# A depthwise 7x7 convolution on TensorE: sixteen small tiles reading the input in place

## The chip, the cores and the metric

The kernel runs on one core of a Trainium2 chip. The metric is the device time of one execution in microseconds (us). A run's engines are TensorE (PE, with its weight loads shown as PEld), VectorE (DVE), ScalarE (ACT), GpSimd (POOL) and SyncE (SP, which only issues transfers here). All data are float32.

## What is computed

The input is 32 images of 96 channels of 56 x 56. Two layers follow each other: a ConvNeXt block (depthwise 7x7 convolution, layer norm over the channels, an MLP of 96 to 384 to 96 with an exact GELU, a residual), and a second layer (depthwise 5x5 convolution, SiLU, a selective scan over the 3136 tokens of an image).

```python
def block(x, conv_w, conv_b, ln_g, ln_b, w1, b1, w2, b2, layer_scale):
    h = depthwise_conv7(x, conv_w) + conv_b              # padding 3
    h = transpose(h, (0, 2, 3, 1))
    h = (h - mean(h)) * rsqrt(var(h) + 1e-5) * ln_g + ln_b   # over the 96 channels
    h = gelu(h @ w1 + b1) @ w2 + b2
    return transpose(h, (0, 3, 1, 2)) * layer_scale + x
def scan_layer(x, ...):
    x = silu(depthwise_conv5(x) + conv_b)                # padding 2
    ...                                                  # projections, softplus, two cumulative sums
```

## The kernel before

Four stages run one after the other, each with its own pools in SBUF and PSUM: first convolution, MLP, second convolution, scan. They hand tensors over in DRAM: `conv1_d` (the convolved channels), `rstd_d` (the norm's reciprocal deviation for each token), `block_d` (the block's output, laid out for the second convolution), `conv2_d`, `du_d`.

**First convolution (L141 to L363).** The images are taken as two halves j of 16 images; a row of an input tile is one image row, with 16 x 56 = 896 values of 16 images behind each other. One job is one channel (the last 16 channels are done half by half): 112 jobs. `load_x` (L156) brings 56 rows of each half. The convolution in the vertical direction is a product with a banded matrix of taps (56 input rows to 56 output rows). Two columns are done together: the even and odd columns of the input stand in `xq` above each other on partitions 0 to 55 and 64 to 119, so that 120 rows are contracted and 112 outputs (two columns x 56 rows) come out. To fill `xq`, every half of a channel is copied out of the loaded tile with a step of two: one copy on POOL or DVE (L328) and one on ACT (L329). Then four horizontal offsets t are accumulated for each half (L334), 8 matmuls of 120 x 112 x 448 a channel. The weights are slices of a tile `wt`, read from the padded table `taps1_d` with two loads a job (`taps_of`, L306), with a step of four elements between columns.

ACT evicts the result with its bias (L343) into `ht`, POOL issues two stores into `conv1_d` (L347), and for the norm DVE subtracts the first channel (L356), adds to a sum (L357), ACT squares (L358), and DVE adds to the sum of squares (L359). `finish_norm(j)` (L126) makes the reciprocal deviation of one half and stores it. The small weights of the later stages are prepared beside the jobs (`beside`, L302); some of them hold a PSUM bank for a few jobs.

**MLP (L369 to L485).** The tokens of 4 image rows of one half and 32 channels make a tile of 128 partitions (`hts`); there are 28 groups n of 4 rows and two parts s (even or odd columns) in each. `hidden` (L413) runs four row tiles of TensorE, 32 x 128 each, `result` (L436) four column tiles, 128 x 32 each. `result` adds bias and residual with two DVE operations of 224 (L451), each picking every fourth column of the input tile `x` and every second value of PSUM, into `ot`, whose last part decides when POOL issues four stores into `block_d` (L463). `normalise` (L410) multiplies a group by `rstd`. In the program's order, the first group's loads come after all first-convolution jobs; a scheduler moves unpinned instructions ahead where buffers and queues allow, while those in `pin(...)` keep the order in which they are written.

**Second convolution and scan (L492 to L868).** The second convolution runs four column tiles of TensorE with a contiguous moving operand, and DVE puts its columns back in order. The scan is DVE's: two scans and one multiply for each of 192 units. Neither stage is touched.

Of the kernel before, what the change touches and what calls it, by code (L numbers as in the profile page):

```python
# [16 lines left out]
ROWS = B2 * H  # L17
# [6 lines left out]
WP = 128  # L24
W2 = W // 2
MP = 64
P1 = (K1 + 1) // 2
# [3 lines left out]
RW = 32  # L31
QP = QW + 1
# [6 lines left out]
EPS = 1e-9  # L39
APART = 16  # L40
# [7 lines left out]
def convnext_then_scan_kernel(  # L48
# [30 lines left out]
    conv1_d = dram.tile([C, ROWS, COLS], F32, name="conv1_d")  # L79
# [3 lines left out]
    rstd_d = dram.tile([ROWS, COLS], F32, name="rstd_d")  # L83
    taps1_d = dram.tile([C, 3 * WP * P1], F32, name="taps1_d")
# [22 lines left out]
    KR = MP + H  # L107
    PQ = HALF

# [8 lines left out]

    front = ctx.enter_context(ExitStack())
    stats = front.enter_context(tc.tile_pool(name="stats", bufs=1))  # L120
    first = stats.tile([ROWS, B2, HALF], F32, name="first")
    acc1 = stats.tile([ROWS, B2, HALF], F32, name="acc1")
    acc2 = stats.tile([ROWS, B2, HALF], F32, name="acc2")
    sq = stats.tile([ROWS, B2, HALF], F32, name="sq")

    def finish_norm(j):  # L126

        a1, a2 = acc1[:, j], acc2[:, j]
        nc.vector.tensor_mul(sq[:, j], a1, a1)
        nc.vector.scalar_tensor_tensor(  # L130
            a2, in0=sq[:, j], scalar=-1.0 / C, in1=a2, op0=ALU.mult, op1=ALU.add
        )
        nc.vector.tensor_scalar(a2, a2, 1.0 / C, 0.0, ALU.mult, ALU.max)
        nc.scalar.activation(a2, a2, AF.Sqrt, bias=eps_t[:ROWS], scale=1.0)
        nc.vector.reciprocal(a1, a2)
        for s in range(2):
            nc.gpsimd.dma_start(
                rstd_d[j * H : (j + 1) * H, s * PQ : (s + 1) * PQ], a1[s * H : (s + 1) * H]
            )

    with tc.tile_pool(name="c1", bufs=3) as pool, tc.tile_pool(  # L141
        name="c1k", bufs=1
    ) as keep, tc.tile_pool(name="prep", bufs=1) as prep, tc.tile_pool(
        name="c1_ps", bufs=4, space=PSUM
    ) as psum:
        wts = [keep.tile([128, 2, H * P1], F32, name=f"wt1_{i}") for i in range(5)]
        xqs = [keep.tile([128, B2, BI, W2 + 3], F32, name=f"xq_{i}") for i in range(3)]
        jobs = [(c, (0, B2)) for c in range(C - APART)]
        jobs += [(c, (j, j + 1)) for j in range(B2) for c in range(C - APART, C)]


        kt1 = prep.tile([C, K1, K1], F32, name="kt1")
        nc.sync.dma_start(kt1, c1w.rearrange("c (i j) -> c i j", j=K1))
        xts: dict = {}

        def load_x(n):  # L156
            c, js = jobs[n]
            xts[n] = pool.tile([128, COLS], F32, name=f"xt1_{n}", tag="xt")
            for j in range(*js):
                nc.sync.dma_start(xts[n][MP * j : MP * j + H], x[c, j * H : (j + 1) * H])  # L160
# [14 lines left out]
        c1b_t = across(c1b, ROWS, C, "c1b_t", const)  # L175
        pad = prep.tile([C, 3, WP, P1], F32, name="pad1")
        nc.vector.memset(pad, 0.0)
        at = H - 1 - K1 // 2
        for i in range(3):
            for t in range(P1):  # L180
                j = 2 * t + 1 - i
                if j in range(K1):
                    nc.vector.tensor_copy(pad[:, i, at : at + K1, t], kt1[:, :, j])
        nc.sync.dma_start(taps1_d, pad.rearrange("c d p t -> c (d p t)"))
        for t in wts + xqs + [acc1, acc2]:
            nc.vector.memset(t, 0.0)
# [119 lines left out]
        def taps_of(n):  # L306

            c, wt = jobs[n][0], wts[n % len(wts)]
            for s in range(2):
                taps = bass.AP(  # L310
                    taps1_d.tensor, taps1_d.offset + (c * 3 + 1 - s) * WP * P1,
                    [[P1, H], [WP * P1, 2], [1, H * P1]],
                )
                nc.sync.dma_start(wt[MP * s : MP * s + H], taps)

        for n in range(4):
            taps_of(n)
        for n, (c, js) in enumerate(jobs):
            if n + 4 < len(jobs):
                taps_of(n + 4)  # L320
            if n + 2 < len(jobs):
                load_x(n + 2)

            xq, xt = xqs[n % len(xqs)], xts.pop(n)
            for j in range(*js):
                xv = xt[MP * j : MP * j + H].rearrange("p (i r s) -> p s i r", i=BI, s=2)
                copy = nc.vector.tensor_copy if j else nc.gpsimd.tensor_copy
                copy(xq[:H, j, :, 2 : W2 + 2], xv[:, 1])  # L328
                nc.scalar.copy(xq[MP:KR, j, :, 1 : W2 + 1], xv[:, 0])  # L329
            wv = wts[n % len(wts)].rearrange("p o m -> p (o m)").rearrange("p (q t) -> p t q", t=P1)  # L330
            ps = bank(f"ps1_{n}")[:ROWS, :, :PQ]
            for t in range(P1):
                for j in range(*js):
                    nc.tensor.matmul(  # L334
                        ps[:, j].rearrange("p (i r) -> p i r", i=BI),
                        lhsT=wv[:KR, t],
                        rhs=xq[:KR, j, :, t : t + W2],
                        start=(t == 0),
                        stop=(t == P1 - 1),
                    )  # L340
            half = slice(*js)
            ht = pool.tile([ROWS, B2, HALF], F32, name=f"ht_{n}", tag="ht") if c else first
            nc.scalar.activation(  # L343
                ht[:, half], ps[:, half], AF.Identity, bias=c1b_t[:, c : c + 1], scale=1.0
            )
            for s in range(2):
                nc.gpsimd.dma_start(  # L347
                    conv1_d[c, js[0] * H : js[1] * H, s * PQ : (s + 1) * PQ].rearrange(
                        "(j m) q -> m j q", m=H
                    ),  # L350
                    ht[s * H : (s + 1) * H, half],
                )
            if c:

                dt = pool.tile([ROWS, B2, HALF], F32, name=f"dt_{n}", tag="dt")
                nc.vector.tensor_sub(dt[:, half], ht[:, half], first[:, half])  # L356
                nc.vector.tensor_add(acc1[:, half], acc1[:, half], dt[:, half])  # L357
                nc.scalar.activation(dt[:, half], dt[:, half], AF.Square)  # L358
                nc.vector.tensor_add(acc2[:, half], acc2[:, half], dt[:, half])  # L359
            if n >= 3 and beside:  # L360
                beside.pop(0)()
            if n == C + 1:
                finish_norm(0)  # L363
# [4 lines left out]

    with tc.tile_pool(name="mlp_ot", bufs=1) as pool_o, tc.tile_pool(  # L369
        name="mlp_g", bufs=14  # L370
    ) as pool_g, tc.tile_pool(name="mlp", bufs=2) as pool, tc.tile_pool(
        name="mlp_h", bufs=3, space=PSUM
    ) as ps_h, tc.tile_pool(name="mlp_o", bufs=2, space=PSUM) as ps_o:
        blocks = C // CB
        rts: dict = {}
        hts: dict = {}
        xts: dict = {}
        gts: dict = {}

        ots = [  # L380
# [532 lines left out]
```

## Time and profile before

| | us |
|---|---|
| median of three runs | 3596.53 (3595.88 to 3597.94) |
| the profiled execution | 3600.45 |
| its span, first to last instruction | 3598.7 |
| mean granted TensorE clock in it | 0.832 |

The profile shows this one execution: for each engine its busy time, groups of equal instructions with their mean duration, and for an engine's idle time the instruction that ended it. Matmuls overlap in TensorE, so the mean duration of one (541 ns) is longer than the distance between two. The transfers by queue:

```profile
q1 hardware_dynamic: 263168, 671.96, 57.9%
q0 software_dynamic: 29632, 80.27, 7.1%
q10 hardware_dynamic: 16904, 38.70, 2.8%
```

Columns: packets, MB, and the time of the packets as a share of 16 DMA engines over the span. q1 is what SP issues, q0 what POOL issues (`conv1_d`, `rstd_d`, `block_d`), q10 what ACT issues. The issues that the change touches, with the number of issues, the size of each, and for POOL's the time to landing:

```profile
block_d<-o POOLq DMA_DIRECT2D x336, 120.0 KB, 5.7
xt<-in_x_dram SPq DMA_DIRECT2D x192, 196.0 KB
x<-in_x_dram SPq DMA_DIRECT2D x336, 112.0 KB
h<-conv_d SPq DMA_DIRECT2D x84, 448.0 KB
```

### The profile page before, as it was taken

To read this page: it belongs to the slowest core of one execution; us is meant where nothing else is said; L and a number is where in the kernel's file an instruction comes from. 1 tells how busy PE (TensorE), PEld (TensorE's weight loads), DVE (VectorE), ACT (ScalarE), POOL (GpSimd) and SP (SyncE) were. 2 spreads that over 40 slices of the span, in tenths; PEclk is the share of its full clock that TensorE was granted. 3 is DMA by queue.
4 is the path that set the end of the run, shared out by engine and by line. 5 is a ranking of instruction groups with operands and counts; after the bars stand their busy time and mean duration, and the time that the engine had idled before them with its cause. 6 is when DMAs were issued, how large, how long until landed. Compare 5 with 4: busy or idle time off the path is not lost. (4 is left out here: it accounts for less than half of the span.)

```text
span 3598.7 us, 46673 instructions
## 1 busy us (share of the span) xinstructions
PE 3053.6 (85%) x17290; PEld 1288.2 (36%) x17290; DVE 2666.7 (74%) x1820; ACT 2352.2 (65%) x2168; POOL 1969.5 (55%) x1284
## 2 busy tenths in 40 slices
PE   8999998999999999899957777777777778777775
PEld 5777775333333333333312222222222222222221
DVE  6666666333333333699959999999999999999998
ACT  4555555333333333588868888888888887888884
POOL 2333343222222222000049899999999998999996
PEclk9999999999999999999966667667666666767666
DMA  6665555444444443699978787778877877877873
GB/s 185 194 179 168 173 168 170 154 158 158 158 157 156 160 157 93 201 283 286 287 222 299 271 266 255 283 253 270 282 256 259 290 255 253 283 255 267 281 259 122
DMA packets 309931, 793.92 MB, mean 221 GB/s; under 512 B 126840, under 2 KB 188304, under 8 KB 285160
## 3 DMA queue, kind: packets, MB, share of 16 engines
q1 hardware_dynamic: 263168, 671.96, 57.9%
q0 software_dynamic: 29632, 80.27, 7.1%
q10 hardware_dynamic: 16904, 38.70, 2.8%
q8 instruction: 137, 2.24, 0.3%
q14 instruction: 90, 0.74, 0.1%
HBM read 555.05 MB, written 235.74 MB: 220 GB/s over the span
## 5 line engine op out<-in xcount | busy, mean ns | idle before, releaser
L711 POOL TENSOR_TENSOR rep<-rep,bt 128x1568 f32<-128x1568 f32 x192 | 674.4, 3513 | 379.8 <-DMA rep<-du_d 379.8
L740 POOL TENSOR_TENSOR hs<-hs,ct 128x1568 f32<-128x1568 f32 x191 | 669.4, 3505 | 102.4 <-DVE hs L728 89.0
L721 DVE TENSOR_TENSOR_SCAN pv<-rep,pv 128x1568 f32<-128x1568 f32 x192 | 664.5, 3461 | 42.8 <-ACT rep L707 24.9
L431 ACT ACTIVATE g<-ph,b1p_t 128x896 f32<-128x896 f32 x336 | 320.0, 1004 | 512.4 <-PE ph L421 512.4
L451 DVE SCALAR_TENSOR_TENSOR o<-po,b2r_t,x 128x224 f32<-128x224 f32 x336 | 190.8, 609 | 567.9 <-PE po L440 567.9
L334 PE MATMUL ps<-xq,wt 120*112 120x448 f32 x1536 | 584.1, 541 | 20.9 <-DMA wt<-taps_d 17.5
L463 POOL DMA_DIRECT2D block_d<-o x336 | 183.1, 552 | 659.2 <-DVE o L451 627.9
L334 PEld LDWEIGHTS ps<-xq,wt 120*112 120x112 f32 x1536 | 429.8, 280 | 173.4 <-issue 22.2
L421 PE MATMUL ph<-h,w1r_t 32*128 32x448 f32 x4032 | 437.8, 558 | 23.7 <-DVE h L411 21.3
L639 PE MATMUL pz<-xs,wd_t 96*96 96x392 f32 x512 | 277.0, 706 | 172.6 <-ACT du L647 126.8
L440 PE MATMUL po<-g,w_t 128*32 128x448 f32 x4032 | 413.1, 543 | 0.0
L758 PE MATMUL py<-hs,sel_t 128*32 128x392 f32 x1536 | 327.5, 682 | 62.7 <-POOL hs L740 62.7
L686 PE MATMUL pk<-bn,pick_t 8*128 8x392 f32 x1024 | 288.5, 683 | 90.7 <-ACT y L767 78.5
L724 DVE SCALAR_TENSOR_TENSOR pv<-pv,rep 128x1568 f32<-128x1568 f32 x192 | 345.6, 1800 | 22.6 <-POOL rep L711 1.6
L533 PE MATMUL ps<-xq,wt 128*32 128x448 f32 x3072 | 309.3, 548 | 38.7 <-DMA xq<-block_d 32.8
L728 DVE TENSOR_TENSOR_SCAN hs<-rep,carry_h,pv 128x1568 f32<-128x1568 f32 x96 | 334.1, 3480 | 10.4 <-DVE pv L724 0.5
L556 DVE COPY st<-yt 28x896 f32<-28x896 f32 x288 | 320.3, 1112 | 28.0 <-ACT yt L547 15.7
L728 DVE TENSOR_TENSOR_SCAN hs<-rep,pv 128x1568 f32<-128x1568 f32 x96 | 328.4, 3420 | 10.3 <-PE pz L639 0.5
L750 PE MATMUL py<-xs,dsm_t 96*96 96x392 f32 x512 | 304.8, 737 | 10.9 <-ACT bn L674 5.4
L706 ACT ACTIVATE rep<-rep,lift_t 128x1568 f32<-128x1568 f32 x192 | 307.6, 1602 | 6.2
L707 ACT ACTIVATE rep<-rep,lift_t 128x1568 f32<-128x1568 f32 x192 | 307.6, 1602 | 6.3
L705 ACT ACTIVATE rep<-rep,a_t 128x1568 f32<-128x1568 f32 x192 | 308.3, 1606 | 3.5 <-DMA rep<-du_d 3.1
(90 smaller groups left out, 3131.0 us busy)
## 6 DMA issues: line engine op xcount, KB each, us to landing
rep<-du_d SPq DMA_DIRECT2D x191, 1568.0 KB
du_d<-du SPq DMA_DIRECT2D x126, 588.0 KB
xq<-block_d SPq DMA_DIRECT2D x192, 225.0 KB
block_d<-o POOLq DMA_DIRECT2D x336, 120.0 KB, 5.7
xt<-in_x_dram SPq DMA_DIRECT2D x192, 196.0 KB
x<-in_x_dram SPq DMA_DIRECT2D x336, 112.0 KB
h<-conv_d SPq DMA_DIRECT2D x84, 448.0 KB
conv_d<-st SPq DMA_DIRECT2D x96, 392.0 KB
```

What stands on the lines that cost most here:

```text
L334: nc.tensor.matmul(ps[:, j].rearrange("p (i r) -> p i r", i=BI), lhsT=wv[:KR, t], rhs=xq[:KR, j, :, t : t + W2], start=(t == 0), stop=(t = ...
L421: pin(nc.tensor.matmul(phs[i // 2][:, i % 2, :HALF], lhsT=w1r_t[rows, d, f * 128 : (f + 1) * 128], rhs=hts[n, d][rows, s * HALF : (s + 1) ...
L431: nc.scalar.activation(gt, ph[:, :, :HALF], AF.Gelu, bias=b1p_t[:, f : f + 1], scale=1.0)
L440: pin(nc.tensor.matmul(po[CB * i : CB * i + CB, :HALF], lhsT=w2_t[:, f, CB * d : CB * d + CB], rhs=gts[n, s, f, i // 2][:, i % 2], start=( ...
L533: pin(nc.tensor.matmul(ps[RW * f : RW * f + RW, h, : B * QW].rearrange("p (b q) -> p b q", q=QW), lhsT=wv[:, f, t], rhs=xv[:, :, t : t + Q ...
L556: pin(copy(st[:, :, :, :, f], yt[RW * f : RW * f + QR].rearrange("p h (b q) -> p h b q", q=QW),))
L711: pin(nc.gpsimd.tensor_mul(ut, ut, bts[i // NG]))
L721: pin(nc.vector.tensor_tensor_scan(grown, da, zero, pv[:, last : last + 1] if q else 1.0 / EPS, ALU.mult, ALU.add))
L724: pin(nc.vector.scalar_tensor_tensor(run, in0=grown, scalar=1.0, in1=ut, op0=ALU.min, op1=ALU.mult))
L728: pin(nc.vector.tensor_tensor_scan(ht, da, run, carry_h[:, col : col + 1] if q else 0.0, ALU.mult, ALU.add))
L740: pin(nc.gpsimd.tensor_mul(ht, ht, cts[k]))
L758: pin(nc.tensor.matmul(py[g * DG : (g + 1) * DG, s, :BK], lhsT=sel_t, rhs=hss[k * NG + g][:, cols], start=False, stop=True, tile_position= ...
```

## The change

**First convolution.** A job is now two channels by two vertical halves h (40 jobs), or four channels by one half (the last 16 channels, 8 jobs). Each of these four inputs k is 32 image rows of all 32 images on 32 partitions (two loads' worth of images side by side, 1792 values); the two vertical halves are 28 output rows each and overlap in their inputs. The 56 columns are split by column modulo 4, f. Each (k, f) is one 32 x 32 tile of TensorE: rows 32k of the input, output partitions 32f of PSUM, 448 tokens (32 images x 14 columns). The seven horizontal taps j are accumulated; each reads the loaded tile itself, every fourth value, from the column group that f + j - 3 falls into. Taps that reach over the image's edge write 13 of 14 columns. There is no `xq` and no copy. The taps come from a smaller table, four loads a job.

The eviction writes two inputs in one operation, the stores are issued by ACT, four a job, and the sums and the square go over the whole job (1792 values). `first`, the sums and the norm have 128 partitions now, with the tokens ordered by half, row, column group. `finish_norm` first adds the two channels' sums.

**MLP.** The tiles of tokens follow the new order: a group is 4 rows of one half and two column groups, and a part is one column group, so each result is one DVE operation of 448 with contiguous PSUM and every fourth value of x. An x tile holds both halves of the images (1792 values) and serves two groups; the output tile holds all four column groups, and its stores come once in two groups, of 7680 bytes a partition. The first rows are loaded and normalised beside the last jobs of the convolution.

The core of the diff:

```diff
-    conv1_d = dram.tile([C, ROWS, COLS], F32, name="conv1_d")
+    conv1_d = dram.tile([C, 2, QR, QC, HALF], F32, name="conv1_d")
...
-    rstd_d = dram.tile([ROWS, COLS], F32, name="rstd_d")
-    taps1_d = dram.tile([C, 3 * WP * P1], F32, name="taps1_d")
+    rstd_d = dram.tile([2, QR, QC, HALF], F32, name="rstd_d")
+    taps1_d = dram.tile([C, TP * K1], F32, name="taps1_d")
...
-        jobs = [(c, (0, B2)) for c in range(C - APART)]
-        jobs += [(c, (j, j + 1)) for j in range(B2) for c in range(C - APART, C)]
+        jobs = [[(c, 0), (c, 1), (c + 1, 0), (c + 1, 1)] for c in range(0, C - APART, 2)]
+        whole = len(jobs)
+        jobs += [
+            [(c + k, h) for k in range(JT)] for h in range(2) for c in range(C - APART, C, JT)
+        ]
...
         def load_x(n):
-            c, js = jobs[n]
-            xts[n] = pool.tile([128, COLS], F32, name=f"xt1_{n}", tag="xt")
-            for j in range(*js):
-                nc.sync.dma_start(xts[n][MP * j : MP * j + H], x[c, j * H : (j + 1) * H])
+            xts[n] = pool.tile([128, 2 * COLS], F32, name=f"xt1_{n}", tag="xt")
+            for k, (c, h) in enumerate(jobs[n]):
+                nc.sync.dma_start(
+                    two(xts[n][RW * k : RW * k + RW]),
+                    x[c].rearrange("(j m) q -> m j q", m=H)[h * (H - RW) : h * (H - RW) + RW],
+                )
...
-            for j in range(*js):
-                xv = xt[MP * j : MP * j + H].rearrange("p (i r s) -> p s i r", i=BI, s=2)
-                copy = nc.vector.tensor_copy if j else nc.gpsimd.tensor_copy
-                copy(xq[:H, j, :, 2 : W2 + 2], xv[:, 1])
-                nc.scalar.copy(xq[MP:KR, j, :, 1 : W2 + 1], xv[:, 0])
...
+        def convolve(n):
+            wv = wts.pop(n).rearrange("p (o j) -> p j o", j=K1)
+            xv = xts.pop(n).rearrange("p (b q f) -> p f b q", q=QW, f=QC)
+            pss = [bank(f"ps1_{n}_{a}") for a in range(JT // 2)]
+
+            order = sorted(range(K1), key=lambda j: j != K1 // 2)
+            for j in order:
+                for f in range(QC):
+
+                    far, g = divmod(f + j - K1 // 2, QC)
+                    lo, hi = max(0, -far), QW - max(0, far)
+                    for k in range(JT):
+                        rows = slice(RW * k, RW * k + RW)
+                        nc.tensor.matmul(
+                            pss[k // 2][RW * f : RW * f + RW, k % 2, :HALF].rearrange(
+                                "p (b q) -> p b q", q=QW
+                            )[:, :, lo:hi],
+                            lhsT=wv[rows, j],
+                            rhs=xv[rows, g, :, lo + far : hi + far],
+                            start=(j == order[0]),
+                            stop=(j == order[-1]),
+                            tile_position=(RW * k, RW * f),
+                        )
+            return pss
...
+            for f in range(QC):
+                if n < whole:
+                    to = conv1_d[c : c + 2, :, :, f].rearrange("a h m q -> m (a h) q")
+                else:
+                    to = conv1_d[c : c + JT, h, :, f].rearrange("a m q -> m a q")
+                nc.scalar.dma_start(to, hs[RW * f : RW * f + QR])
...
+            for ks, a1, _ in parts:
+                nc.vector.tensor_add(a1, a1, flat(dt[:, ks]))
+            nc.scalar.activation(dt, dt, AF.Square)
+            for ks, _, a2 in parts:
+                nc.vector.tensor_add(a2, a2, flat(dt[:, ks]))
...
+            if n == len(jobs) - 3:
+                load_rows(0)
+                load_rows(1)
+            if n == len(jobs) - 2:
+                for d in range(blocks):
+                    normalise(0, d)
...
-            for e in range(2):
-                pin(nc.vector.scalar_tensor_tensor(
-                    ot[:, 2 * e + s, :, e : e + QW],
-                    in0=po[:, :HALF].rearrange("p (i a e) -> p e i a", i=BI, e=2)[:, e],
-                    scalar=b2r_t[:, d : d + 1],
-                    in1=xts[n, d].rearrange("p (i a e s) -> p s e i a", i=BI, s=2, e=2)[:, s, e],
...
+            pin(nc.vector.scalar_tensor_tensor(
+                ot[:, f].rearrange("p (b r) -> p b r", r=QP)[:, :, at : at + QW],
+                in0=po[:, :HALF].rearrange("p (b q) -> p b q", q=QW),
+                scalar=b2r_t[:, d : d + 1],
+                in1=xts[n // 2, d].rearrange("p (b q f) -> p f b q", q=QW, f=QC)[:, f],
```

## The prediction

> **What bounds the kernel now.** I read the slices first, then a table of stages, then the groups by shape, then the timeline inside the first stage. In the slices, PE is full from the start to about 1450 us, and from there DVE is.
>
> ```profile
> PE   8999998999999999899957777777777778777775
> DVE  6666666333333333699959999999999999999998
> ACT  4555555333333333588868888888888887888884
> PEclk9999999999999999999966667667666666767666
> ```
>
> I cut the stages by the first and last matmul of each source line. Columns: length, then busy us (instructions) of PE, PEld, DVE, ACT, POOL, then clock, DMA share, GB/s.
>
> ```profile
> 17.50:606.30 588.80, 585.37 (x1546) 431.14 (x1546) 366.19 (x468) 307.51 (x413) 192.15 (x315) 1.00 0.60 180
> 612.80:1457.90 845.10, 827.79 (x8064) 304.10 (x8064) 276.47 (x420) 322.00 (x338) 183.34 (x333) 1.00 0.46 147
> 1470.20:1806.00 335.80, 309.33 (x3072) 132.33 (x3072) 314.96 (x283) 271.32 (x191) 0.00 (x0) 0.99 0.92 280
> 1885.00:3598.70 1713.70, 1295.05 (x4494) 406.94 (x4492) 1642.93 (x567) 1397.43 (x1179) 1546.76 (x591) 0.67 0.77 261
> ```
>
> The first convolution (588.8 us) and the MLP (845.1 us) are PE's; the second convolution and the scan, which the diff leaves alone, are 2.1 ms that stay. So the question is what one pair of channels costs PE. The groups by shape give the durations used below (the last column before the idle time is the mean ns):
>
> ```profile
> L334 PE MATMUL ps<-xq,wt 120*112 120x448 f32 x1536 | 584.1, 541 | 20.9 <-DMA wt<-taps_d 17.5 <-ACT xq L329 3.4
> L334 PEld LDWEIGHTS ps<-xq,wt 120*112 120x112 f32 x1536 | 429.8, 280 | 173.4 <-issue 22.2 <-ACT xq L329 4.0
> L421 PEld LDWEIGHTS ph<-h,w1r_t 32*128 32x128 f32 x4032 | 189.8, 186 | 273.2 <-issue 154.2 <-ACT g L431 84.4 <-DVE h L411 34.7
> L533 PEld LDWEIGHTS ps<-xq,wt 128*32 128x32 f32 x3072 | 132.3, 141 | 215.8 <-issue 186.2 <-ACT st L556 23.5 <-DMA xq<-block_d 3.7
> L440 PEld LDWEIGHTS po<-g,w_t 128*32 128x32 f32 x4032 | 114.3, 109 | 274.0 <-issue 239.5 <-DVE h L411 34.5
> L356 DVE TENSOR_TENSOR dt<-ht,first 112x896 f32<-112x896 f32 x79 | 86.3, 1092 | 55.5 <-ACT ht L343 55.2
> L343 ACT ACTIVATE ht<-ps,c1b_t 112x896 f32<-112x896 f32 x79 | 79.6, 1008 | 12.6 <-PE ps L334 12.1
> ```
>
> 768 f32 matmuls stand in the program and 1536 in the trace: each is two passes. In steady state one pass starts every 0.376 us (266 in 100 us), so two channels cost 2 x 8 x 2 x 0.376 = 12.0 us.
>
> The timeline of one channel shows the loop that would bind next: DVE's second sum waits for ACT's square.
>
> ```profile
> 301.63 1.09 DVE L357 TENSOR_TENSOR acc<-acc,dt 112x896 f32<-112x896 f32 x1
> 302.82 0.95 ACT L358 ACTIVATE dt<-dt 112x896 f32<-112x896 f32 x1 [1.71 <-DVE acc L357]
> 303.80 1.09 DVE L359 TENSOR_TENSOR acc<-acc,dt 112x896 f32<-112x896 f32 x1 [1.08 <-ACT dt L358]
> ```
>
> **What the Trainium skill says.** "TensorE: Matmul & The Clock Gate", Measured speedup vs the span model: sixteen 32x32 tiles together gave 10.6x. The trace has only four tiles, and there it agrees with packing: the MLP starts 8064 passes in 845 us, one in 105 ns against 94 = 376/4. "SBUF — State Buffer", Door 1: 16-byte lines, at least two reads of a line are needed for full rate. The trace agrees for weights. Contiguous loads of 128 and 32 columns take 186 and 109 ns: 0.80 ns a column and 83 ns fixed. The load at L334 steps 16 bytes a column and takes 280: (280 - 83)/112 = 1.76 ns; that at L533 steps 32 bytes: (141 - 83)/32 = 1.8 ns. No matmul of before reads its moving operand in steps, so for that no run shows it yet. "TensorEngine Tiling (Array Packing)", Gotcha 1: row tiles must not share a PSUM bank; the change gives each of the four k its own, as L421 does for its four row tiles.
>
> **The change part by part.**
>
> PE. A job is two channels by two halves: 7 taps x 4 columns f x 4 inputs k = 112 matmuls, 224 passes, 14 for each of 16 tiles. 40 jobs of two channels and 8 of four channels by one half: 48. Of a tile's 7 taps 3 reach over the edge and stream 416 columns, not 448. What a pass costs is the choice. Its moving operand is now `xt` itself, every fourth element: 16 bytes a step.
> - Floor: unchanged rate, 0.376 us; a job is 2 x (4 x 0.376 + 3 x 0.349) = 5.1 us.
> - Half rate, as the weights show: 1.68 (twice 376/448) to 1.8 ns a column. I take 1.72: 0.770 and 0.716 us, a job 2 x (4 x 0.770 + 3 x 0.716) = 10.5 us; ends 10.2 and 11.0.
>
> I take the half rate, because an 8-fold or 4-fold column step slows a load alike, and because the four stepped loads of L533 run side by side with 1.8 ns each, no worse than the lone one of L334: four streams don't crowd each other. Issue should keep up: the trace has 16 PE instructions passing between two semaphore marks in 75 ns, and a job needs 448 in 10.5 us (23 ns each).
> Sum: 48 x 10.5 = 502, plus 3 for the jobs in which ps_w1 holds a bank; 505 against 588.8.
>
> ACT and DVE. The copies go: L329 (607 ns, x192), L328 on DVE (415, x96) and POOL (621, x96). They lie under PE, worth nothing by themselves. Shapes double to 1792 elements: from 1.09 and 0.63 us for 896 and 448, one DVE operation is 2.03; the square, from 0.95 and 0.58, is 1.70; eviction stays 2 x 1.01. Loop of a job: sub 2.03 + sum 2.03 + square 1.70 + second sum beside the next eviction 2.03 + three handovers of 0.1 = 8.1 us; a half job with its four short sums and evictions 8.9. Under 10.5, so hidden; with PE at its floor this binds.
>
> Queues. The stores of conv1_d move from POOL to ACT, four a job at 0.3 to 0.6 us of issue (ACT's own issues in the opening): some 2 us while DVE sums; behind them waits only the square, which waits for the sum anyway. SP issues 4 taps and 4 loads at about 0.4: 3 us a job. Bytes a job: x 917 KB, taps 115, stores 803 = 1.84 MB; in 10.5 us 175 GB/s, near today's 180; at 8.1 us 227, below the 280 of the second convolution.
>
> Start. Pad is filled in one copy, not ten, and taps1_d is 183 KB, not 590 (before, issue at 7.65, first use at 14.25). But eight loads of 229 KB stand ahead of it. Between -5 and +2: I take -2.
>
> MLP. Same matmuls. L451 becomes one operation of 448 instead of two of 609 ns; between 0.6 and 1.1 us, on an engine busy a third. Normalising the first rows now comes before the last sums, so PE needn't wait for DVE as it did (6.5 us), but ACT must do the last square, swap tables for a square root between the first two steps' GELUs (two loads of 1.28), and load_x(0) waits for the released tiles: -4 to +6, taken +1. At the end four stores of 245 KB per block follow the last result instead of 123: 0 to +6 before the second convolution's loads, taken +2.
>
> Sum: -84 - 2 + 1 + 2 = -83 us. The profiled execution took 3600.45 (span 3598.7), the median is 3596.53, 3.9 lower; I carry the difference to the median: 3513.5, said as 3513.
>
> **Rivals.**
> A. Stepped moving reads cost nothing. For it: a weight load and a moving stream are different ports. Against: both take about 0.8 ns a column when contiguous and pass through the same memory. PE then needs 5.1, the DVE-ACT loop binds: 40 x 8.1 + 8 x 8.9 = 395 against 588.8, -194 + 1: 3404 (3385 to 3440).
> B. The forecast: half rate, sixteen together: 3513 (3488 to 3550).
> C. The slow side: half rate, and sixteen tiles don't stay full. Each tile's two passes follow each other in program order, so PE must look past a waiting second pass to the next tile. In the trace PE's semaphore marks run ahead of the matmuls begun by at most 23 matmuls; four tiles need only 7 ahead, sixteen need 31. If it holds eight tiles busy, a job is 20.9 us: 48 x 20.9 = 1004, +415: 4012. It decides from 12.2 us a job (588.8/48), that is below 13.7 tiles busy. For it: nothing here has more than four. [...]Eight tiles at full rate would look like B in time.
> That the program doesn't do what it says is excluded by its order: PE's list holds 5376 of the small matmuls.
>
> **Numbers.** A 0.25, B 0.55, C 0.20. Within 0.2% (7 us), what a measurement of this kernel can tell from no change: 0.01, out of C. Faster 0.79, slower 0.20. The range takes A and B and the stretch just above B: 3385 to 3600.
>
> **What would show it.** Busy PE at clock 1.00 through the first stage and a job of 112 matmuls every 10.5 us: B. PE with holes of 3 us a job and DVE near 75%: A. Starts of one tile over 0.8 us apart while others idle: C. A weight load of about 141 ns, L451's successor under 1.1 us, and a stage of MLP within 10 us of 845 check the rest. It fails if the stepped rate is neither 1 nor 1/2, or if the MLP pays for tokens in their new order.

## The result and the profile after

The changed kernel takes 3606.80 us (median of seven runs), the kernel before 3597.43 in the runs beside it: a ratio of 1.0021, 95% interval 1.0009 to 1.0032. It is slower by a fifth of a per cent, where 83 us less were forecast. The profiled execution took 3605.23 us, its span 3603.4.

The slices of the changed kernel, the same four rows that the prediction shows for the kernel before:

```profile
PE   7999997999999999899957777777787777778775
DVE  4555555333333333699959999999999999999998
ACT  1233332433333333588868888888888888888885
PEclk9999998999999999999967667667667667666666
```

DVE and ACT became lighter in the first six slices, as the copies went, and PE stayed full at its full clock: the engine that binds is the same, and it got no less to do in time. The table of stages, cut as in the prediction (length, busy us and instructions of PE, PEld, DVE, ACT, POOL, clock, DMA share, GB/s):

```profile
21.80:606.50 584.70, 577.34 (x10762) 536.16 (x10762) 296.07 (x172) 171.69 (x156) 2.23 (x4) 0.99 0.55 157
606.50:617.40 10.90, 0.02 (x3) 0.05 (x4) 5.38 (x6) 3.79 (x5) 0.00 (x0) 0.65 0.40 111
617.40:1466.00 848.60, 829.43 (x8064) 304.02 (x8064) 265.38 (x261) 326.21 (x341) 88.67 (x171) 0.99 0.46 148
1466.00:1477.00 11.00, 0.05 (x4) 0.08 (x6) 4.66 (x9) 0.00 (x0) 3.03 (x7) 0.68 0.95 303
1477.00:1810.60 333.60, 309.11 (x3072) 132.63 (x3072) 316.31 (x284) 272.54 (x191) 0.00 (x0) 0.99 0.93 282
```

Against the stages before: start 21.8 instead of 17.5 (+4.3), first convolution 584.7 instead of 588.8 (-4.1), gap 10.9 instead of 6.5 (+4.4), MLP +3.5, next gap -1.3, second convolution -2.2. That is +4.6, and the spans differ by 4.7. So the question is the first convolution: -4 where -84 was forecast.

The groups of its steady part, from 100 to 500 us:

```profile
L355 PE MATMUL ps<-xt,wt 32*32 32x448 f32 x4319 | 399.9, 982 | 0.0
L355 PEld LDWEIGHTS ps<-xt,wt 32*32 32x32 f32 x7529 | 380.3, 145 | 18.1 <-issue 1.1 <-DVE wd_t L303 0.2
L355 PE MATMUL ps<-xt,wt 32*32 32x416 f32 x3233 | 361.2, 939 | 0.0
L417 DVE TENSOR_TENSOR acc<-acc,dt 128x1792 f32<-128x1792 f32 x34 | 68.9, 2026 | 62.1 <-ACT dt L415 62.1
```

A matmul of 448 columns lasts 982 ns here and 541 before. No idle time stands before the two shapes of matmul: PE is never without one in flight. One job in the timeline:

```profile
300.78 1.90 ACT L377 ACTIVATE hs<-ps,c1b_t 128x896 f32<-128x896 f32 x2 [3.90 <-PE ps L355]
302.71 2.03 DVE L402 TENSOR_TENSOR dt<-hs,first 128x1792 f32<-128x1792 f32 x1 [3.78 <-ACT hs L377]
304.77 2.03 DVE L414 TENSOR_TENSOR acc<-acc,dt 128x1792 f32<-128x1792 f32 x1
306.83 1.70 ACT L415 ACTIVATE dt<-dt 128x1792 f32<-128x1792 f32 x1 [4.15 <-DVE acc L414]
308.57 2.02 DVE L417 TENSOR_TENSOR acc<-acc,dt 128x1792 f32<-128x1792 f32 x1 [1.77 <-ACT dt L415]
312.74 1.01 ACT L377 ACTIVATE hs<-ps,c1b_t 128x896 f32<-128x896 f32 x1 [4.20 <-PE ps L355]
```

ACT waits for PE ahead of both evictions, which are 11.96 us apart; the mean over the steady jobs, from the first pass of one to the first of the next, is 11.9. Two channels cost 12.0 before. Sixteen small tiles with slow reads are worth just what one large tile with fast reads was.

### The profile page after: what moved, and what is told of

The parts are those of the page before. It is cut to its first block, busy times and chain, and to the rows that moved or that the text cites. A ratio compares the mean times of both kernels' runs of the same rounds, so it can differ in the third digit from the quotient of the medians.

```text
span 3603.4 us, 62478 instructions
## 1 busy us (share of the span) xinstructions
PE 3045.5 (85%) x26506; PEld 1391.5 (39%) x26506; DVE 2580.6 (72%) x1370; ACT 2222.5 (62%) x1915; POOL 1678.0 (47%) x799
## 5 line engine op out<-in xcount | busy, mean ns | idle before, releaser
L355 PE MATMUL ps<-xt,wt 32*32 32x448 f32 (+1 forms) x10752 | 575.8, 964 | 29.1 <-DMA wt<-taps_d 21.8
L513 DVE SCALAR_TENSOR_TENSOR o<-po,b2r_t,x 128x448 f32<-128x448 f32 x168 | 170.9, 1017 | 579.2 <-PE po L500 547.9
L355 PEld LDWEIGHTS ps<-xt,wt 32*32 32x32 f32 x10752 | 534.8, 145 | 65.7 <-issue 27.8
L524 POOL DMA_DIRECT2D block_d<-o x168 | 81.2, 490 | 750.2 <-DVE o L513 587.4
```

Of the source, the lines that this page charges most:

```text
L355: nc.tensor.matmul(pss[k // 2][RW * f : RW * f + RW, k % 2, :HALF].rearrange("p (b q) -> p b q", q=QW)[:, :, lo:hi], lhsT=wv[rows, j], rhs ...
```

## The experiments

Two theories stood at the start. S: what a pass costs is the step of its moving operand, whatever the number of tiles. R: sixteen tiles get in each other's way (issue, weights, or streams on the same partitions), and the step matters little. Diffs are against the changed kernel unless said. "Job" is the mean time from the first pass of one job to that of the next in the steady part of the stage.

**The same work without the step.**

```diff
-            xv = xts.pop(n).rearrange("p (b q f) -> p f b q", q=QW, f=QC)
+            xv = xts.pop(n).rearrange("p (f b q) -> p f b q", q=QW, f=QC)
```

> Changes the values of the first convolution: each tile still streams 448 or 416 values of its input rows, but values that lie next to each other instead of every fourth one (so other columns of the image are multiplied). Everything else is as in the changed kernel. Theory S (the stepped moving read is what a pass costs, whatever the number of tiles): a pass falls back to about 0.38 us, PE would need 5 to 6 us a job, the DVE-ACT loop of 8.1 us a job binds, the first convolution takes 395 to 410 us instead of 585 and the whole about 3425. Theory R (sixteen tiles crowd each other in issue, weights or columns, the step is free): a job stays near 12 us and the whole near 3605.

3488.5 us; the stage in the windows view:

```profile
21.80:473.50 451.70, 368.40 (x10762) 265.06 (x10762) 290.16 (x169) 167.76 (x154) 2.23 (x4) 0.94 0.71 203
```

133 us shorter, with PE busy 368 of 452 us where it was busy all the time. This is what S says, but the expected 395 to 410 was not reached: 26 of the first 43 jobs take 7.8 to 8.3 us from square to square, the loop over DVE and ACT, and the others up to 13. What holds those is followed up below.

**The step halved, to 8 bytes.**

```diff
-            xv = xts.pop(n).rearrange("p (b q f) -> p f b q", q=QW, f=QC)
+            xv = xts.pop(n).rearrange("p (g b q f) -> p g f b q", q=QW, f=2, g=2)
-                            rhs=xv[rows, g, :, lo + far : hi + far],
+                            rhs=xv[rows, g // 2, g % 2, :, lo + far : hi + far],
```

> Changes the values of the first convolution: the moving operand is read in steps of 8 bytes (two values of each 16), not 16 (other columns of the image are multiplied). If the price is one 16-byte line for each value that is used, with two values of a line enough for the full rate: as without a step, the DVE-ACT loop binds, first convolution 395 to 410 us, whole about 3425. If any step costs the half rate: 585 us and 3605. If the price is by bytes passed over: a pass of about 0.55 us, PE 7.5 to 8 us a job, close to the loop, about 400 to 430 us. Theory R: 585 us.

3472.8 us, stage 447.0: no slower than contiguous, and like it short of the expected 395 to 410. So the price is not for a step as such, nor for bytes passed over: it comes between 8 and 16 bytes, where one value of each 16 is read and no longer two (12 bytes were not tried). PE does not bind in these two runs, so the stage alone does not give the pass. Where PE is supplied, 64 passes in a row start one in 28.5 ns with contiguous reads and one in 30.3 ns with steps of 8 bytes (the lower tenth, from 100 to 400 us): 6% more, and not the double. The Trainium skill ("SBUF — State Buffer", Door 1) asks for two reads in each 16-byte line for the full rate; this run agrees, for TensorE's moving operand.

**The lone tile with the step.** The kernel before, its copied columns spread to 16 bytes each:

```diff
-        xqs = [keep.tile([128, B2, BI, W2 + 3], F32, name=f"xq_{i}") for i in range(3)]
+        xqs = [keep.tile([128, B2, BI, W2 + 3, 4], F32, name=f"xq_{i}") for i in range(3)]
-                        rhs=xq[:KR, j, :, t : t + W2],
+                        rhs=xq[:KR, j, :, t : t + W2, 0],
```

> Computes the reference. The kernel before, with its single 120 x 112 tile, whose copied columns are written and read with 16 bytes from value to value; nothing else differs. Theory S: a lone pass of 448 columns takes 0.75 to 0.82 us instead of 0.376, the first convolution 1150 to 1270 us instead of 589, the whole about 4170 to 4280. Theory R: the pass stays at 0.376 us while copies with stepped writes stay hidden, the whole 3600 to 3640.

4239.4 us. The group of its matmuls over the whole run:

```profile
L334 PE MATMUL ps<-xq,wt 120*112 120x448 f32 x1536 | 1211.8, 967 | 18.1 <-DMA wt<-taps_d 17.9
```

1211.8 us for 1536 passes, back to back: 0.789 us each, against 0.376 contiguous. That is 1.76 ns a column, and it settles what the step alone costs, without a second tile in sight. By this rate a job of sixteen tiles would take 2 x (4 x 0.789 + 3 x 0.733) = 10.7 us. It takes 11.9. S explains most of it, and 1.15 us a job is left.

**Eight or twelve tiles.** After the first tap only some tiles go on: two of four column groups, two of four inputs, or three of four inputs.

```diff
-                for f in range(QC):
+                for f in range(QC if j == order[0] else 2):
...
-                    for k in range(JT):
+                    for k in range(JT if j == order[0] else 2):
...
-                    for k in range(JT):
+                    for k in range(JT if j == order[0] else 3):
```

> Leaves out six of the seven taps for the column groups f = 2 and 3, so that after the first tap only eight of the sixteen tiles work; the two groups that stay do what they did, all else is as in the changed kernel. A lone pass in 16-byte steps was 0.789 us (1211.8 us for 1536). Theory S (each stream pays for its own step): a working tile still needs fourteen passes of about 0.79 us in each job, 11.0 us; if sixteen tiles lose nothing by their number the job stays where it was, 11.9; the whole 3560 to 3605. Theory R (streams that read the same partitions share a rate): the pass halves, the job falls to the DVE-ACT loop of about 8 us and the whole to 3450 to 3490.

> Leaves out six of the seven taps for the inputs k = 2 and 3, so that after the first tap eight tiles work: two row groups by four column groups, where the run with two column groups had four by two. All else as in the changed kernel. If the last 1.0 us of a job comes from the number of passes in flight: job 10.9 us as there, whole about 3560. If it comes from four streams that read the same partitions: job 11.8, whole about 3600. If from streams that end in the same columns' partitions: 10.7 to 10.9, as by number; this run alone doesn't tell these two apart.

> Leaves out six of the seven taps for the input k = 3, so that twelve tiles work after the first tap. All else as in the changed kernel. If the cost grows with the number of tiles: job 11.3 to 11.5 us, between 11.0 with eight and 11.85 with sixteen, whole 3575 to 3592. If it is a limit that only sixteen reach: 11.0, whole 3560 to 3582.

The job, between 300 and 420 us, was 10.9 us with two column groups, 11.0 with two inputs, 11.0 with three inputs (whole: 3560.1, 3582.0, 3573.7 us; the second loses 26 us between the convolution and the MLP, so the jobs are compared and not the whole). Half or three quarters of the tiles save most of the excess over the lone rate's 10.7, and no more. R's large form is out: streams on the same partitions don't share a rate, since four streams a row group (second run) go as fast as two (first run). And the excess does not grow in step with the tiles: 0.2 to 0.3 us a job with eight or twelve, 1.15 with sixteen.

**The order, and the weights.** The first edit lets every column group take its short taps last, the second exchanges the two inner loops, the third reads the weights contiguous.

```diff
+            own = [sorted(order, key=lambda j: (j != K1 // 2, short(f, j))) for f in range(QC)]
...
-                for f in range(QC):
+                for k in range(JT):
+                    for f in range(QC):
...
-            wv = wts.pop(n).rearrange("p (o j) -> p j o", j=K1)
+            wv = wts.pop(n).rearrange("p (j o) -> p j o", j=K1)
```

> Computes the reference. The changed kernel with the taps of each column group in an order of its own, so that the three taps of 416 columns come last in every group, together; before, every round of sixteen had some passes of 416 and some of 448. If PE's order of start holds all tiles to the pace of the slowest in a round, a job falls by three rounds of two passes times 0.056 us, 0.33 us, and the stage by 16 us: 3585 to 3595. If tiles run on their own: no change, 3603 to 3610.

> Computes the reference. The changed kernel with its two inner loops exchanged: the four column groups of an input follow each other, not the four inputs of a column group. If the last 1.0 us of a job comes from the number of tiles alone: job 11.85, whole 3600 to 3612. If neighbours in the order that read the same partitions block each other: job over 12.2, whole over 3620. If the order before was the bad one: job 10.9 to 11.4, whole 3560 to 3590.

> Changes the values of the first convolution: the weights of a tile are read contiguous (other taps of the table), not in 28-byte steps; the input is still read in 16-byte steps, all else as in the changed kernel. A job takes 11.85 us there, with eight working tiles 10.9, by the lone rate 10.7. If the loads of sixteen tiles' weights (145 ns each) are what costs the last 1.0 us: 109 ns a load, job 10.9 to 11.3 us, whole 3560 to 3585. If not: job 11.8, whole 3600 to 3612.

Short taps last: job 11.9, 3604.9 us, ratio to before 1.0020 (1.0012 to 1.0028), as the changed kernel. Loops exchanged: job 11.9, 3609.3. Neither the pace of the slowest in a round nor the neighbour in the order matters. The trace of the first run also shows that PE starts passes out of the program's order: all passes of 448 columns of a job stand ahead of those of 416 there, and around the change 8 to 17 starts in each job are mixed. Weights contiguous: their loads fall from 145 to 103 ns and the job by 0.25 us, 3596.4 us. So a fifth of the excess goes with the time of the weight loads, less than half of what that run expected at the least; the rest has no cause shown.

**Who issues the stores.**

```diff
-                nc.scalar.dma_start(to, hs[RW * f : RW * f + QR])
+                nc.gpsimd.dma_start(to, hs[RW * f : RW * f + QR])
```

> Computes the reference. The changed kernel with the four stores of conv1_d of a job issued by GpSimd, as before the change, and not by ACT. If ACT's issue, held for 24 us when the first rows of the MLP are loaded, is what held PE for 7 to 9 us and lengthened the gap before the MLP: 3592 to 3600. If the loads themselves take the time: 3603 to 3610.

3590.5 us, ratio to before 0.9982 (0.9975 to 0.9988): 16 us less than the changed kernel. The timeline of the changed kernel near the end of the stage shows what was removed:

```profile
556.90 19.81 SPq L158 DMA_DIRECT2D h<-conv_d  x7
565.88 23.96 ACTq L390 DMA_DIRECT2D conv_d<-hs  x4
568.65 2.22 DVE L414 TENSOR_TENSOR acc<-acc,dt 128x896 f32<-128x896 f32 x2
589.88 1.70 ACT L415 ACTIVATE dt<-dt 128x1792 f32<-128x1792 f32 x1 [24.03 <-DMA h<-conv_d]
592.67 8.27 PE L355 MATMUL ps<-xt,wt 32*32 32x448 f32 x124 [7.27 <-ACT hs L377]
```

SP has issued seven loads of 448 KB for the MLP; ACT's four stores, issued in 2.6 us elsewhere, now take 24. DVE has long summed (570.9), but the square waits behind ACT's issue until 589.9, the eviction behind the square, and PE 7.3 us for a free bank. The same place with GpSimd's stores:

```profile
569.37 2.39 POOL L390 DMA_DIRECT2D conv_d<-hs  x4
571.25 1.70 ACT L415 ACTIVATE dt<-dt 128x1792 f32<-128x1792 f32 x1 [5.12 <-DVE acc L414]
```

The square follows the sum, PE runs through (574.95 of 575.00 us busy), the stage is 9.7 us shorter and the gap before the MLP 4.2 us instead of 10.9.

**GpSimd undoes the step.**

```diff
+            xq = pool_o.tile([128, QC, HALF], F32, name=f"xq1_{n}", tag="xq", bufs=2)
+            nc.gpsimd.tensor_copy(xq, xts.pop(n).rearrange("p (n f) -> p f n", f=QC))
+            xv = xq.rearrange("p f (b q) -> p f b q", q=QW)
```

> Computes the reference. GpSimd copies each job's input once so that the four column groups lie one behind the other, and the sixteen tiles read contiguous values; all else is as in the changed kernel. Theory S: PE needs 5 to 6 us a job, the copy 2.5 to 4 us of GpSimd lies beside other work, the DVE-ACT loop of 8.1 us a job binds: first convolution 395 to 420 us, whole 3415 to 3440, against before 0.950 to 0.957. Theory R: a job stays near 12 us, whole 3605 or more.

3540.2 us, ratio 0.9842 (0.9826 to 0.9859): faster than both kernels, but at least 100 us above what was expected. The timeline of this run:

```profile
194.60 5.11 POOL L345 COPY xq<-xt 128x1792 f32<-128x1792 f32 x1 [8.03 <-PE ps L357]
196.16 5.45 DVE L404 TENSOR_TENSOR dt<-hs,first 128x1792 f32<-128x1792 f32 x1
```

The copy ends at 199.71. DVE's difference, 2.03 us elsewhere, begins at 196.16 and ends 1.9 us after the copy: it stood still while the copy ran. Of 45 operations of DVE that begin during a copy, 43 end 1.9 us after it. It goes the other way too: copies that begin beside no operation of DVE take 3.3 to 3.9 us, those that begin during one up to 5.3. The Trainium skill has it ("SBUF — State Buffer", SBUF: two separate sides): a DVE operation with two inputs in SBUF and a GpSimd operation that reads SBUF exclude each other. The trace agrees; the expectation forgot it, and the copy went into the loop it was to lie beside: DVE is busy 406 us of this stage, against 290 in the contiguous run.

**Other column groups, no copy.** The four groups become two halves of the row by parity. Then the tiles read in steps of 8 bytes, and the MLP writes each result with two operations of 224.

```diff
-            xv = xts.pop(n).rearrange("p (b q f) -> p f b q", q=QW, f=QC)
+            xv = xts.pop(n).rearrange("p (b q s) -> p s b q", q=W // 2, s=2)
...
-                    far, g = divmod(f + j - K1 // 2, QC)
-                    lo, hi = max(0, -far), QW - max(0, far)
+                    at, g = divmod(f % 2 + j - K1 // 2, 2)
+                    at += f // 2 * QW
+                    lo, hi = max(0, -at), min(QW, W // 2 - at)
...
-                            rhs=xv[rows, g, :, lo + far : hi + far],
+                            rhs=xv[rows, g, :, lo + at : hi + at],
```

> Computes the reference. The four column groups are two halves of the row by parity instead of column modulo 4, so that tiles read the loaded input in steps of 8 bytes, at the full rate shown with other columns; the MLP's result is two operations of 224 with their own place in the output, as before the change. All else is as in the changed kernel. Theory S: job near 7.8 us where the DVE-ACT loop binds, more where ACT's stores wait for their issue; first convolution 440 to 455 us, whole 3465 to 3495. Theory R: 3600.

3465.7 us, ratio 0.9634 (0.9618 to 0.9650); stage 443.5, job 8.8, as expected. This is the change's plan at the price that it needed.

**Then the stores back to GpSimd, and the sums rearranged.** The first run adds to the last one the stores of `conv1_d` and of `taps1_d` on GpSimd. The second moves a job's square and second sum behind the first sum of the next job, the third pins that order, the fourth has six buffers and loads five jobs ahead.

```diff
-        nc.sync.dma_start(taps1_d, pad.rearrange("c p j -> c (p j)"))
+        nc.gpsimd.dma_start(taps1_d, pad.rearrange("c p j -> c (p j)"))
...
-            nc.scalar.activation(dt, dt, AF.Square)
-            for ks, _, a2 in parts:
-                nc.vector.tensor_add(a2, a2, flat(dt[:, ks]))
+            squares()
+            late.append((dt, [(a2, flat(dt[:, ks])) for ks, _, a2 in parts]))
...
-                nc.scalar.activation(dt, dt, AF.Square)
+                pin(nc.scalar.activation(dt, dt, AF.Square))
...
-            if n + 3 < len(jobs):
+            if n + 5 < len(jobs):
```

> Computes the reference. The version with two halves by parity, with the stores of conv1_d and the one store of taps1_d issued by GpSimd; so ACT's square waits for no issue, and the taps' table is not behind eight input loads. If the jobs of 8.6 to 13 us in that version come from ACT held in its issues: job 7.8 to 8.1 us throughout, first convolution 390 to 410 us, start at 14 to 18 us instead of 21.8, whole 3405 to 3440. If from the transfers themselves: first convolution 430 to 445, whole 3450 to 3465.

> Computes the reference. As the run before it, and the square and the second sum of a job come after the first sum of the next job, so that DVE doesn't wait for ACT between its two sums. The loop of 8.1 us falls to DVE's own 6.1 us; PE's passes at the full rate have shown jobs of 6.5 to 7.3 us, the transfers of 1.84 MB need 6.6 us at 280 GB/s. First convolution 330 to 375 us, whole 3350 to 3405. If something else than that loop holds the jobs of the run before: no change against it.

> Computes the reference. As the run with late squares, whose engine lists had the old order all the same (square and second sum of a job before the next job's difference); now evictions, sums and squares are pinned in the order written. If the loop over DVE and ACT holds the jobs of 8.1 us: DVE's three operations of 2.03 remain, 6.1 us, PE and transfers need 6.3 to 7.2; first convolution 330 to 370 us, whole 3360 to 3410. If it is PE or the transfers: no change, 3440 to 3460.

> Computes the reference. As the run with the pinned order, with six tiles of input and of taps instead of four, filled five jobs ahead instead of three. If the holes between jobs are loads that were issued too late: jobs of 7.0 to 7.5 us, first convolution 370 to 395 us, whole 3405 to 3430. If PE's rate of starting small passes or the transfers' rate holds it: within 10 us of 3451.

| run | us | ratio to before | stage | job |
|---|---|---|---|---|
| stores on GpSimd | 3449.37 | 0.9580 (0.9560 to 0.9599) | 415.9 | 8.5 |
| late squares | 3459.64 | 0.9613 (0.9597 to 0.9628) | 415.0 | 8.5 |
| the same, pinned | 3451.37 | 0.9598 (0.9582 to 0.9614) | 414.2 | 8.5 |
| loads further ahead | 3455.49 | 0.9607 (0.9591 to 0.9624) | 418.9 | 8.6 |

The stores were worth 28 us of stage, 18.6 of them in the last two jobs (26.0 us between their first passes with ACT's stores, 7.4 with GpSimd's). That is less than expected, and only 16 us of it reached the whole: the gap before the MLP grew from 13.0 to 20.0 us, and DVE waits there for the loads of the first rows. The three versions after it brought nothing more; their gaps are 27.3, 24.1 and 23.8 us. The late squares were no test: the scheduler put each square before the next eviction again, the old order. Pinned, the order is the written one, and DVE no longer waits between its sums. From one job to the next in the pinned run, DVE and PE alone:

```profile
252.74 2.02 DVE L415 TENSOR_TENSOR acc<-acc,dt 128x1792 f32<-128x1792 f32 x1
253.10 4.54 PE L356 MATMUL ps<-xt,wt 32*32 32x416 f32 x128 [1.07 <-issue]
254.69 2.02 DVE L426 TENSOR_TENSOR acc<-acc,dt 128x1792 f32<-128x1792 f32 x1
259.71 2.02 DVE L403 TENSOR_TENSOR dt<-hs,first 128x1792 f32<-128x1792 f32 x1 [3.01 <-ACT hs L378]
259.96 12.63 PE L356 MATMUL ps<-xt,wt 32*32 32x448 f32 x331 [2.32 <-issue]
```

DVE's second sum follows the first at once, and then DVE is idle 3 us. The job is no shorter, so that loop was no longer what held it. PE is near: where it is supplied, 64 passes in a row start one in 31 to 35 ns (the lower tenth and the median over the steady part), which makes 7.0 to 7.8 us of 224 passes. The rest of the 8.5 us are holes of 0.3 to 2.9 us in which no pass starts, 45 us in 300. Loading further ahead did not fill them.

What ends them can be read from the trace. The profile has a queue named `instruction` (packets, MB, share of 16 engines):

```profile
q8 instruction: 208, 3.41, 0.4%
```

These are 208 packets of 16 KB. The kernel before, with 9216 passes fewer, has 137, and in the pinned run one comes for each 127 passes: they bring PE's program. Between 100 and 400 us that run has 31 holes over 0.45 us, and 29 of them, 36.6 of 38.4 us, end 1.2 to 1.6 us after such a packet has landed. The two holes above end at 253.10 and 259.96; the packets ahead of them landed at 251.71 and 258.69. With the stores on GpSimd it is 28 of 31, with loads further ahead 30 of 34, and in the contiguous run at the start 36 of 37.

So by the traces PE waits in these versions for its own instructions and not for data; with the loads further ahead, the input of a job is asked for some 40 us before its first pass, and the holes stay. No run changed the supply of instructions, so this cause is read and not tested. Why a packet comes late stays open, and the transfers' rate (221 GB/s in that stretch, 157 in the stage of the changed kernel) may have a part in it. It is not the changed kernel's excess of 1.15 us: with slower passes the same packets come in time there, and its stretch has one hole over 0.45 us where the pinned run has 31.

## Why the prediction failed

*What a pass costs.* The branch was right: weight loads and moving reads, both at about 0.8 ns a column when contiguous, pay alike for the step. The value was a little low: 1.72 ns a column was taken, 1.76 measured on a lone tile, inside the two ends of 1.68 and 1.8. A job is 10.71 instead of 10.46 us by it: 12 us of the stage.

*Sixteen tiles at once.* This is the step that failed. The forecast took all sixteen tiles as always full, and so put the loss from running them together at nothing, while the rival C took eight; there was no case between. Measured is 10.71 us of work in 11.87 us, as much as 14.4 of 16 tiles always busy: 48 x 1.16 = 56 us, the largest term. (Whether tiles wait between passes or passes last longer among sixteen, the trace does not tell, since the ends of matmuls are modelled in it.) C named the mechanism (tiles don't stay full), a cause for it (PE's look past a waiting pass), and the point from which it decides, 12.2 us a job; the job came within 0.3 us of that point. The cause that C gave isn't shown: PE does start passes out of order, eight and twelve tiles run at 10.9 to 11.0, the order of the tiles doesn't matter, shorter weight loads give back a fifth, the remainder is open.

The Trainium skill ("TensorE: Matmul & The Clock Gate", Measured speedup vs the span model) was cited there for the packing, with 10.6x for sixteen tiles. The forecast took from it that sixteen run together, and not a number below sixteen. In the runs with cheap reads the traces come near that number: 224 passes, 81.6 us one after the other (2 x 16 x (4 x 0.376 + 3 x 0.349)), take 7.0 to 7.8 us, 10.5 to 11.7 at once. So case A's floor of 5.1 us a job for PE was too low as well. The quotient of 16 PE instructions in 75 ns was a burst: sustained it is 31 to 35 ns for a weight load and its pass, 16 to 18 for each. That is still under the 23 ns that the forecast needed, so issue does keep up with half-rate passes; with case A's 5.1 us, 11 ns each, it would not.

*Queues.* "Behind them waits only the square, which waits for the sum anyway" holds in a steady job, where the four issues take 2.6 us. It fails where the loads of the MLP are in flight: 24 us of issue on ACT, the square late, PE 7.3 us without a bank. The first passes of the last two jobs are 20.4 us apart, 8.5 more than elsewhere, and the gap is 6.7 longer than with GpSimd's stores, which save 16 us of the whole; by this alone the sign of the result is decided (0.9982 against 1.0021).

*The stage's sum:* 12 + 56 + 8.5, and 2 in three longer jobs near its start (13.0, 14.2 and 13.3 us, 5 us in all where 3 were put in), are 78.5 of the 79.7 us between 505 forecast and 584.7 measured.

*Start.* -2 was taken from -5 to +2, +4.3 came, outside these ends. The reason was named and priced too low:

```profile
1.21 12.78 SPq L187 DMA_DIRECT2D xt<-in_x_dram  x8
15.31 0.33 SPq L209 DMA_DIRECT2D taps_d<-pad  x1
19.77 5.80 SPq L336 DMA_DIRECT2D wt<-taps_d  x12
21.84 9.06 PE L355 MATMUL ps<-xt,wt 32*32 32x448 f32 x135 [21.84 <-DMA wt<-taps_d]
```

`pad` was ready at 3.85, but SP needs 12.8 us to issue the eight loads ahead of its store: eight at the 0.4 us of a short load were 3.2. With the store on GpSimd the first matmul came at 20.1, since the loads of the taps, issued from 14.9 on, still stand behind those of the input.

*MLP and what is around it.* The forecast's +1, from -4 to +6, took in the gap before the stage. Gap and stage are 4.4 and 3.5 us longer, 7.9 together and outside these ends. With the stores on GpSimd (gap 4.2, stage 850.5) they are 3.1 longer together, so what is too much comes from ACT's issue. The gap before the second convolution got shorter by 1.3, where +2 was taken, from 0 to +6. L451's successor was bounded by 0.6 and 1.1 us:

```profile
L513 DVE SCALAR_TENSOR_TENSOR o<-po,b2r_t,x 128x448 f32<-128x448 f32 x168 | 170.9, 1017 | 579.2 <-PE po L500 547.9 <-DMA x<-in_x_dram 15.0 <-issue 8.5
```

1017 ns, the upper end: the one wide operation with a step of 16 bytes is little better than two of 609. Engine durations (2.03, 1.70, 1.00 us, weight loads of 145 ns) came as forecast.

*The range* reached to 3600 and the measurement lies 7 us above. With a case for 13 to 15 busy tiles, between B and C, it would have held it. A result at the edge of no change (0.21% against the forecast's 0.2%) would then not have stood at 0.01.

## What to carry to other kernels

Before a copy in front of TensorE is traded for a strided read, count how many values of each 16 bytes the stream uses: two cost next to nothing here, one halved the rate, and the grouping of the columns could be chosen to use two. When many small tiles are to run at once, take the measured concurrency as a factor of the sum, with a case below it, and not the number of tiles. When an issue is moved to an engine that also computes, look for the place where the queues are full, not for the mean time of an issue. And when passes become many and short, look for gaps between their starts that end soon after a packet of the queue `instruction`, before shortening anything else.

## What the runs showed of the hardware

- A moving operand of float32 in 16-byte steps streams at 1.76 ns a column on a lone tile (0.789 us for 448), a contiguous one at 0.84 (0.376 us). In 8-byte steps sixteen tiles start a pass every 30.3 ns where they are supplied, contiguous every 28.5 (lower tenth).
- Sixteen tiles of 32 x 32 with passes of 0.79 us do the work of 14.4 tiles that are always busy; with passes of about 0.38 us PE starts one in 31 to 35 ns, as if about 11 ran at once.
- PE starts passes out of the program's order: 8 to 17 starts are mixed where the program changes from 448 to 416 columns.
- PE's program comes in packets of 16 KB, one for about 127 passes with their weight loads. At 31 to 35 ns a pass, 29 of 31 longer holes in PE end 1.2 to 1.6 us after such a packet (36.6 us in 300); at 53 ns a pass one such hole is left in the same stretch.
- Four transfers of 196 KB that ACT issues in 2.6 us took 24 us to issue while seven loads of 448 KB on SP's queue were under way.
- A GpSimd copy of 128 x 1792 (3.3 to 3.9 us alone) and DVE's operations with two inputs stop each other: 43 of 45 of DVE's that began during a copy ended 1.9 us after it.
